# A written order for the first layer's cross-attention and shared expert, on all engines and over eight PSUM banks in turn

## The chip, the cores and the metric

The kernel runs on one core of a Trainium2 chip. A core has five engines that run side by side, each taking its own instructions strictly in the order in which they are queued: TensorE (PE: matrix multiplications and transposes; its weight loads are shown as PEld), VectorE (DVE), ScalarE (ACT), GpSimd (POOL) and SyncE (SP, which here only starts DMA transfers). They work on an on-chip memory, SBUF, and TensorE writes its results to a second one, PSUM, of eight banks, from which DVE or ACT read them. Engines wait for each other by semaphores. The metric is the time of one execution on the device in microseconds (us), median of three runs.

## The reference, cut to what matters

The reference is a two-layer decoder in float32 on 64 sequences of 64 positions with 128 features. Each layer has self-attention, cross-attention with a context of the same shape, and a feed-forward network of experts. The change lies in the first layer's cross-attention and in the part of its expert network that follows at once. Cut to that:

```
# x: 64 x 64 x 128; context: the same shape; 16 heads of 64
lat = layer_norm(layer_norm(x)) * g2 + b2       # x is normalised outside too
ctx = layer_norm(context) * g1 + b1
q   = lat @ Wq;   k, v = split(concat([ctx, lat], axis=1) @ Wkv)
w   = softmax(q k^T / 8)                        # 64 queries, 128 keys, 16 heads, per sequence
x   = x + (w v) @ Wout

h      = layer_norm(x)
probs  = softmax(rms_norm(h) @ router_w.T)      # 8 experts, the best two are taken
routed = each expert's silu(h rg) * (h ru) @ rd on at most 640 of its rows, weighted, added back
shared = (silu(h @ sg) * (h @ su)) @ sd         # 1024 hidden features, all rows
x      = x + shared + routed
```

## The kernel before

The 4096 rows are held in SBUF as eight tiles `xres[g]` of 128 partitions by 4 by 128 (a group g is eight sequences). The program has four stages, each with its own pools of SBUF and PSUM: the first layer's self-attention and dense experts (A), the stage of this change (X), the eight routed experts of the first layer one after the other (B), and the second layer (C).

**Stage X for a group.** The context rows are loaded by SP into `cg` (`load`, L912). `latent_rows` and `context_rows` normalise the rows: statistics on DVE (`ln_stats`, L154 and L155), the inverse root as a power on POOL (`inv_sqrt`, L163), a subtraction and multiplication for each 128 rows on DVE (L175). The latents go through two roots, since they are normalised twice. `keys_by_feature` transposes four tiles of 128 by 128 on TensorE (`transpose4`, L67) and ACT scales them into `kvT`; `keys_by_row` transposes back into `kvN`. Query and key weights are folded beforehand into `wqk`, value and output weights into `wvo`, so that `queries` makes for two heads of four sequences a piece of `qx` from the latents (matmuls `xq`, ACT copy L960), and `scores` multiplies the queries of eight heads of one sequence with its keys (matmuls `sc`, four products of 128 by 128 in one bank). The softmax: DVE takes the negative maximum and adds it (L976, L978), ACT the exponential (L979), DVE the sum and its reciprocal (L981, L982), POOL the multiplication (L983). `keys_first` transposes the result (`pt_p`) and ACT copies it to `pT` (L990); `sums` weights the keys' rows with it (`pu`, copied to `uT` by ACT, L1004); `output` adds 16 heads' products with `wvo` for two sequences (`pz`) and DVE adds them to `xres` (L1017). So a group has 16 pieces each of `queries`, `scores`, `keys_first` and `sums`, and four of `output`.

Then `ffn_rows` normalises the new rows into `xf`, `ffn_features` transposes them into `xfT`, `ffn_route` computes the router's logits (`rl`), the two best experts and their weights in some twenty small DVE operations, and the running count of rows for each expert; `ffn_places` turns these, with a matmul over earlier rows (`pp`), into the row's place in a DRAM table, `sidx`. `dispatch` scatters 128 rows to that table by two indirect DMAs on POOL's queue (L1097), one for each chosen expert. `shared` makes 128 of the shared expert's 1024 hidden features (matmuls `gg_s` and `gu_s`, tanh on ACT L1118, two DVE operations L1119 and L1120 into `sh`), eight pieces for a group, and `shared_out` multiplies 128 rows with `sd` (`sp`) and adds them to `xres` (L1133).

**What sets the order.** `at(slot, place, f, ...)` enters a piece in a list; `run_todo` calls all pieces by slot and place and, while it runs, `mm` and `transpose` keep TensorE's instructions in that order. In stages A and C `eng.pin()` does the same for DVE, ACT and POOL, and slots come from long tables of times written in the code. In stage X the slots are eight to a group (one for each sequence, with twelve places in each), in a regular pattern: scores of sequence b one slot before its transposes and sums, the next group's queries six slots ahead, the routed part of a group in the slots after its last output. Only TensorE is held to this order there; the instructions of DVE, ACT and POOL are put in an order by the framework's scheduler, and so is each of them against the others.

**Banks and buffers.** `psum_pool(pa, "psX", mm=3, sc=2, tp=1, av=2)` gives stage X three banks for queries, outputs, shared pieces and the router, two for scores, one for all transposes and two for `sums`. With `turns=True`, as in stage A, banks of a kind are taken strictly in turn. Buffers in SBUF that matter: `cg` 1, `p` (the softmax tile) 3, `pT` 2, `uT` 2, `qx` 2, `kvT` 2, `sh` 3, `th` 2.

**The stage's end.** Stage B's first load (`rg`, L1181) and its rows `xe` (L1188, read from the scattered table) stand on SP's queue.

Of the kernel before, what the change touches and what calls it, by code (L numbers as in the profile page):

```python
# [7 lines left out]
F32 = mybir.dt.float32  # L8
# [8 lines left out]
P = 128  # L17
D = 128
# [36 lines left out]
def decoder(ctx: ExitStack, tc: tile.TileContext, io: dict, out: bass.AP):  # L55
# [123 lines left out]
    def transpose4(src, nm):  # L179
        n = min(src.shape[1], TG)  # L180
        pt = psum("tp" if "tp" in banks else "mm", [P, TG, P], f"pt_{nm}")[:, 0:n]
        for i in range(n):
            transpose(pt[:, i, :], src[:, i, :], ident)
        return pt
# [714 lines left out]
    with ExitStack() as pa:  # L899
        psum_pool(pa, "psX", mm=3, sc=2, tp=1, av=2)  # L900
# [5 lines left out]

        run = sm.tile([P, E1], F32, tag="run", name="run")
        nc.vector.memset(run, 0.0)
# [4 lines left out]

        def latent_rows(s):

            g, x4 = s.g, xres[s.g]
            mv = ln_stats(sm, x4, f"l{g}")
            r = inv_sqrt(sm, mv[:, :, 1], EPS, f"l{g}")
            v2 = var_after(sm, mv[:, :, 1], r, f"l{g}")
            r2 = inv_sqrt(sm, v2, EPS, f"l2{g}")  # L920
            nc.vector.tensor_tensor(out=r2, in0=r2, in1=r, op=ALU.mult)
            s.ll = fk.tile([P, TG, D], F32, tag="ll", name=f"ll_{g}")
            normalise(s.ll, x4, mv, r2)

        def context_rows(s):
            g = s.g
            mv = ln_stats(sm, s.cg, f"c{g}")
            r = inv_sqrt(sm, mv[:, :, 1], EPS, f"c{g}")
            s.cn = fk.tile([P, TG, D], F32, tag="cn", name=f"cn_{g}")
            normalise(s.cn, s.cg, mv, r)  # L930

        def keys_by_feature(s, k):

            if k:
                s.kvT = fk.tile([P, 8, 2, S], F32, tag="kvT", name=f"kvT_{s.g}", bufs=2)
            pt = transpose4(s.ll if k else s.cn, f"{'l' if k else 'c'}{s.g}")
            nc.scalar.activation(
                s.kvT[:, :, k, :],
                split_b(pt),
                AF.Identity,  # L940
                scale=lnv[:, 2 * k : 2 * k + 1],
                bias=lnv[:, 2 * k + 1 : 2 * k + 2],
            )

        def keys_by_row(s, h):

            if h == 0:
                s.kvN = fk.tile([P, 8, D], F32, tag="kvN", name=f"kvN_{s.g}", bufs=2)
            pt = transpose4(s.kvT[:, 4 * h : 4 * h + 4].rearrange("p b c t -> p b (c t)"), f"n{s.g}_{h}")
            nc.scalar.copy(s.kvN[:, 4 * h : 4 * h + 4, :], pt)  # L950

        def queries(s, hg, h):

            if h == 0:
                s.qx[hg] = big.tile([P, 4, 16, S], F32, tag="qx", name=f"qx_{s.g}_{hg}", bufs=2)
            lat = s.kvT[:, 4 * hg : 4 * hg + 4, 1, :]
            pq = psum("mm", [P, 2, 4, S], f"xq_{s.g}_{hg}_{h}")
            for j in range(2):
                mm(pq[:, j], lhsT=wqk[:, h + j, :], rhs=lat, start=True, stop=True)
            nc.scalar.copy(s.qx[hg][:, :, h : h + 2, :].rearrange("p b h q -> p h b q"), pq)  # L960

        def scores(s, b, hf):
# [3 lines left out]
            psc = psum("sc", [P, 4, P], f"sc_{nm}")  # L966
            for j in range(4):
# [6 lines left out]
                )  # L974
            nmx = sm.tile([P, 4], F32, tag="nmx", name=f"nmx_{nm}", bufs=4)
            nc.vector.tensor_reduce(out=nmx, in_=psc, axis=AX, op=ALU.max, negate=True)  # L976
            pr = wk.tile([P, 4, P], F32, tag="p", name=f"p_{nm}", bufs=3)
            nc.vector.tensor_tensor(out=pr, in0=psc, in1=bcast(nmx, P), op=ALU.add)  # L978
            nc.scalar.activation(pr, pr, AF.Exp, scale=0.125)  # L979
            rc = sm.tile([P, 4], F32, tag="rc", name=f"rc_{nm}", bufs=4)  # L980
            nc.vector.tensor_reduce(out=rc, in_=pr, axis=AX, op=ALU.add)  # L981
            nc.vector.reciprocal(rc, rc)  # L982
            nc.gpsimd.tensor_tensor(out=pr, in0=pr, in1=bcast(rc, P), op=ALU.mult)  # L983
            s.pr[b, hf] = pr

        def keys_first(s, b, hf):
            nm = f"{s.g}_{b}_{hf}"
            pt = transpose4(s.pr[b, hf], f"p{nm}")
            s.pT[hf] = wk.tile([P, 4, P], F32, tag="pT", name=f"pT_{nm}", bufs=2)
            nc.scalar.copy(s.pT[hf], pt)  # L990

        def sums(s, b, hf):

            if b % 2 == 0 and hf == 0:
                s.uT[b // 2] = wk.tile([P, 16, 2, S], F32, tag="uT", name=f"uT_{s.g}_{b // 2}")
            pu = psum("av", [P, 8, S], f"pu_{s.g}_{b}_{hf}")
# [3 lines left out]
                rhs=s.pT[hf].rearrange("p j t -> p (j t)"),  # L1000
# [3 lines left out]
            nc.scalar.copy(s.uT[b // 2][:, 8 * hf : 8 * hf + 8, b % 2, :], pu)  # L1004

        def output(s, i):
            pz = psum("mm", [P, D], f"pz_{s.g}_{i}")
# [9 lines left out]
            nc.vector.tensor_tensor(out=xt, in0=pz, in1=xt, op=ALU.add)  # L1017

        def ffn_rows(s):
            g, x4 = s.g, xres[s.g]  # L1020
            mv = ln_stats(sm, x4, f"f{g}")
            r = inv_sqrt(sm, mv[:, :, 1], EPS, f"f{g}")
            s.xf = io_p.tile([P, TG, D], F32, tag="xf", name=f"xf_{g}")
            normalise(s.xf, x4, mv, r)
            s.rr = inv_sqrt(sm, var_after(sm, mv[:, :, 1], r, f"f{g}"), EPS32, f"f2{g}")

        def ffn_features(s):
            pt = transpose4(s.xf, f"f{s.g}")
            s.xfT = fk.tile([P, TG, P], F32, tag="xfT", name=f"xfT_{s.g}", bufs=2)
            nc.scalar.copy(s.xfT, pt)  # L1030

        def ffn_route(s):

            g = s.g
            ts_ = slice(TG * g, TG * g + TG)
            pl = psum("mm", [P, TG, E1], f"rl_{g}")
            for i in range(TG):
                mm(pl[:, i, :], lhsT=s.xfT[:, i, :], rhs=rwT, start=True, stop=True)
            lg = sm.tile([P, TG, E1], F32, tag="lg", name=f"lg_{g}")
            nc.vector.tensor_tensor(out=lg, in0=pl, in1=bcast(s.rr, E1), op=ALU.mult)  # L1040
            e = exp_shifted(sm, lg, E1, f"f{g}")
            top = sm.tile([P, TG, 2], F32, tag="top", name=f"top_{g}")
            nc.vector.tensor_reduce(out=top[:, :, 0], in_=e, axis=AX, op=ALU.max)
            oh1 = first_max(sm, e, top[:, :, 0], E1, f"f1{g}")
            nc.vector.scalar_tensor_tensor(e, oh1, -2.0, e, ALU.mult, ALU.add)
            nc.vector.tensor_reduce(out=top[:, :, 1], in_=e, axis=AX, op=ALU.max)
            oh2 = first_max(sm, e, top[:, :, 1], E1, f"f2{g}")
            tot = sm.tile([P, TG], F32, tag="tot", name=f"tot_{g}")
            nc.vector.tensor_tensor(out=tot, in0=top[:, :, 0], in1=top[:, :, 1], op=ALU.add)
            nc.vector.reciprocal(tot, tot)  # L1050

            nc.vector.tensor_scalar(tot, tot, 0.5, None, ALU.mult)
            nc.vector.tensor_tensor(out=wtop[:, ts_, :], in0=top, in1=bcast(tot, 2), op=ALU.mult)

            s.oh = (oh1, oh2)
            s.msk = sm.tile([P, TG, E1], F32, tag="msk", name=f"msk_{g}")
            nc.vector.tensor_tensor(out=s.msk, in0=oh1, in1=oh2, op=ALU.add)
            s.before = sm.tile([P, TG, E1], F32, tag="before", name=f"before_{g}")
            nc.vector.tensor_copy(s.before[:, 0, :], earlier[0])
            for i in range(TG - 1):  # L1060
                nc.vector.tensor_tensor(
# [3 lines left out]
            nc.vector.tensor_tensor(out=run, in0=s.before[:, TG - 1, :], in1=s.msk[:, TG - 1, :], op=ALU.add)  # L1065
            earlier[0] = run

        def ffn_places(s):

            g = s.g  # L1070
            ts_ = slice(TG * g, TG * g + TG)
            pp = psum("mm", [P, TG, E1], f"pp_{g}")
            mm(pp, lhsT=cst[:, C_ST : C_ST + P], rhs=s.msk, start=True, stop=False)
            mm(pp, lhsT=ones, rhs=s.before, start=False, stop=True)
            kp = sm.tile([P, TG, E1], F32, tag="kp", name=f"kp_{g}")
            nc.vector.tensor_scalar(kp, pp, float(CAP), None, ALU.is_lt)
            sl = sm.tile([P, TG, E1], F32, tag="sl", name=f"sl_{g}")
            nc.vector.tensor_tensor(
# [3 lines left out]
            nc.vector.tensor_tensor(out=sl, in0=sl, in1=bcast(tr, E1), op=ALU.subtract)  # L1082
            nc.vector.tensor_tensor(out=sl, in0=sl, in1=kp, op=ALU.mult)
            for k, oh in enumerate(s.oh):
                nc.vector.tensor_tensor(out=oh, in0=oh, in1=sl, op=ALU.mult)
                si = sm.tile([P, TG], F32, tag="si", name=f"si_{g}_{k}")
                nc.vector.tensor_reduce(out=si, in_=oh, axis=AX, op=ALU.add)
                nc.vector.tensor_tensor(out=si, in0=si, in1=tr, op=ALU.add)
                nc.vector.tensor_copy(sidx[:, ts_, k], si)
                nc.vector.tensor_scalar(si, si, float(NSLOT), None, ALU.min)  # L1090
                nc.vector.tensor_copy(gidx[:, ts_, k], si)
# [15 lines left out]
        def shared(s, c):  # L1107

            if c % 4 == 0:
                s.hid[c // 4] = big.tile([P, 4, 512], F32, tag="hid", name=f"sh_{s.g}_{c // 4}", bufs=3)  # L1110
            rhs = s.xfT.rearrange("p i t -> p (i t)")
            pg = psum("mm", [P, 512], f"gg_s{s.g}_{c}")
            mm(pg, lhsT=sg[:, c * P : (c + 1) * P], rhs=rhs, start=True, stop=True)
            pu = psum("mm", [P, 512], f"gu_s{s.g}_{c}")
# [3 lines left out]
            nc.scalar.activation(th, pg, AF.Tanh, scale=0.5)  # L1118
            nc.vector.scalar_tensor_tensor(th, th, 1.0, pg, ALU.add, ALU.mult)  # L1119
            nc.vector.tensor_tensor(out=s.hid[c // 4][:, c % 4, :], in0=th, in1=pu, op=ALU.mult)  # L1120

        def shared_out(s, i):
            pe = psum("mm", [P, D], f"sp_{s.g}_{i}")
# [9 lines left out]
            nc.vector.scalar_tensor_tensor(xt, pe, 0.5, xt, ALU.mult, ALU.add)  # L1133


        (X_S0, X_Q0, X_T0, X_S1, X_G, X_T1, X_U0, X_Q1, X_U1, ONE_T, X_Z, ONE_M) = range(12)
        earlier = [run]
        for g in range(NG):
            s = Group()
            s.g, s.qx, s.pr, s.pT, s.uT, s.hid = g, {}, {}, {}, {}, {}  # L1140
            t = 8 * g
            at(t - 12, X_S0, load, s)
            at(t - 10, X_G, latent_rows, s)
            at(t - 9, X_G, context_rows, s)
            at(t - 8, ONE_T, keys_by_feature, s, 1)
            at(t - 7, ONE_T, keys_by_feature, s, 0)
            at(t - 6, ONE_T, keys_by_row, s, 0)
            at(t - 5, ONE_T, keys_by_row, s, 1)
            for hg in range(2):
                for h in range(0, 16, 2):  # L1150
                    at(t - 6 + 4 * hg + h // 4, X_Q1 if h % 4 else X_Q0, queries, s, hg, h)
            for b in range(8):
                for hf, (sc, tr, su_) in enumerate(((X_S0, X_T0, X_U0), (X_S1, X_T1, X_U1))):
                    at(t + b - 1, sc, scores, s, b, hf)
# [1058 lines left out]
```

## Time and profile before

| what | value |
|---|---|
| time, median of 3 runs | 1911.66 us (1910.52 to 1919.04) |
| profiled execution | 1925.23 us, span 1923.5 us |
| mean granted TensorE clock | 0.976 |
| busy in the span | PE 95%, PEld 72%, DVE 64%, ACT 50%, POOL 30% |
| stage X, first context statistics to last shared output | about 442 to 1177 us |
| stage B's first TensorE instruction | 1183.09 us |

Times in the trace are microseconds from the start of the span. A line of TensorE gives the start, the length, the operation and its tiles, how many instructions were merged (x), and in brackets how long the engine stood idle before it and what ended that. A matmul in float32 shows as two instructions. A TensorE piece's length includes the time until its last result has drained; the next piece starts before that, so the difference of two starts tells what a piece costs. Idle time of the other engines costs nothing where TensorE is not made to wait.

### The profile page before, as it was taken

To read this page: it belongs to the slowest core of one execution; us is meant where nothing else is said; L and a number is where in the kernel's file an instruction comes from. 1 tells how busy PE (TensorE), PEld (TensorE's weight loads), DVE (VectorE), ACT (ScalarE), POOL (GpSimd) and SP (SyncE) were. 2 spreads that over 40 slices of the span, in tenths; PEclk is the share of its full clock that TensorE was granted. 3 is DMA by queue.
4 is the path that set the end of the run, shared out by engine and by line. 5 is a ranking of instruction groups with operands and counts; after the bars stand their busy time and mean duration, and the time that the engine had idled before them with its cause. 6 is when DMAs were issued, how large, how long until landed. Compare 5 with 4: busy or idle time off the path is not lost.

```text
span 1923.5 us, 42409 instructions
## 1 busy us (share of the span) xinstructions
PE 1833.8 (95%) x17390; PEld 1378.1 (72%) x17390; DVE 1224.6 (64%) x3492; ACT 959.2 (50%) x1743; POOL 586.4 (30%) x600
## 2 busy tenths in 40 slices
PE   8999999997999999999999998998999999999998
PEld 6666667676877777777878775774777776777775
DVE  5566666636675766666556754554587687676678
ACT  2444444444554454445454432335577666666553
POOL 1111111102234242423223231006575554543332
PEclk9799999998999999999999998998899999999999
DMA  8000000000000000000000002321000100100000
GB/s 284 16 2 2 1 2 2 2 1 17 7 6 12 6 12 9 9 12 6 6 2 4 1 3 83 109 62 33 20 13 13 18 16 16 17 9 8 8 2 18
DMA packets 39791, 41.67 MB, mean 22 GB/s; under 512 B 4501, under 2 KB 31445, under 8 KB 39340
## 3 DMA queue, kind: packets, MB, share of 16 engines
q1 hardware_dynamic: 29100, 27.40, 4.6%
q0 software_dynamic: 4096, 6.83, 1.6%
q10 hardware_dynamic: 6400, 4.72, 0.8%
q8 instruction: 137, 2.24, 0.5%
q14 instruction: 58, 0.48, 0.1%
HBM read 28.97 MB, written 11.53 MB: 21 GB/s over the span
## 4 chain that ended last, share of the span: by engine, by line
PE 78%; DVE 11%; issue 4%; POOL 2%; ACT 2%; DMA 1%; ACTq 0%; SPq 0%; POOLq 0%; DVEq 0%
PE sc L64 6%; PE pz L64 6%; PE pu L64 5%; PE xq L64 5%; PE down L64 5%; PE ph L64 5%; PE py L64 3%; PE xqT L64 3%; PE pt_p L67 2%; DVE x L80 2%; PE xz L64 2%; PE sp L64 2%; PE ey L64 2%; PE gg_s L64 2%; PE gu_s L64 2%
## 5 line engine op out<-in xcount | busy, mean ns | idle before, releaser
L983 POOL TENSOR_TENSOR p<-p,rc 128x512 f32<-128x512 f32 x128 | 133.2, 1044 | 297.2 <-DVE rc L982 100.2
L64 PEld LDWEIGHTS down<-w2T,hid 128*128 128x128 f32 x1024 | 129.5, 191 | 44.9 <-DVE x L80 21.6
L960 ACT COPY qx<-xq 128x512 f32<-128x512 f32 x128 | 74.6, 583 | 159.1 <-PE xq L64 158.7
L80 ACT ACTIVATE hid<-ph,wa 128x512 f32<-128x512 f32 x128 | 85.7, 686 | 135.3 <-PE ph L64 135.0
L64 PE MATMUL down<-w2T,hid 128*128 128x128 f32 x1024 | 139.7, 279 | 2.5 <-DVE x L80 2.0
L64 PE MATMUL pu<-pT,kvN 128*128 128x512 f32 x256 | 131.8, 598 | 6.3 <-ACT pT L990 6.2
L64 PE MATMUL sc<-kvT,qx 128*128 128x128 f32 x1024 | 136.4, 276 | 0.0
L64 PE MATMUL ph<-hT,w1T 128*128 128x512 f32 x256 | 133.1, 618 | 0.1
L64 PE MATMUL xq<-kvT,wqk 128*128 128x256 f32 x512 | 132.6, 384 | 0.6
L64 PEld LDWEIGHTS sc<-kvT,qx 128*128 128x128 f32 x1024 | 125.4, 192 | 4.5 <-issue 2.6
L64 PEld LDWEIGHTS pz<-wvo,uT 128*128 128x128 f32 x1024 | 118.4, 192 | 9.1 <-issue 6.2
L64 PEld LDWEIGHTS xq<-kvT,wqk 128*128 128x128 f32 x512 | 93.4, 193 | 37.0 <-issue 25.8
L64 PE MATMUL pz<-wvo,uT 128*128 128x128 f32 x1024 | 119.5, 275 | 0.0
L976 DVE TENSOR_REDUCE nmx<-sc 128x4 f32<-128x512 f32 x128 | 88.0, 687 | 48.9 <-PE sc L64 47.9
L1323 POOL DMA_INDIRECT yk<-y_dram,gidx x64 | 65.3, 1021 | 150.6 <-DMA y_dram<-ye 134.3
L990 ACT COPY pT<-pt_p 128x512 f32<-128x512 f32 x128 | 74.2, 580 | 69.5 <-PE pt_p L67 68.7
L979 ACT ACTIVATE p<-p 128x512 f32<-128x512 f32 x128 | 80.7, 631 | 45.8 <-DVE p L978 33.9
L1097 POOL DMA_INDIRECT xg_dram<-xf,sidx x64 | 63.7, 995 | 121.0 <-DVE si L1090 47.5
L80 POOL TENSOR_TENSOR p_x<-p_x,nmx_x 128x512 f32<-128x512 f32 x64 | 65.4, 1043 | 99.9 <-DVE nmx_x L80 96.9
L80 DVE SCALAR_TENSOR_TENSOR x<-ey,oh_e,x 128x128 f32<-128x128 f32 x256 | 88.8, 348 | 9.4 <-PE ey L64 2.1
L1017 DVE TENSOR_TENSOR x<-pz,x 128x128 f32<-128x128 f32 x32 | 9.3, 292 | 132.8 <-PE pz L64 132.8
L981 DVE TENSOR_REDUCE rc<-p 128x4 f32<-128x512 f32 x128 | 87.0, 680 | 8.7 <-ACT p L979 6.4
(327 smaller groups left out, 4255.0 us busy)
## 6 DMA issues: line engine op xcount, KB each, us to landing
xg_dram<-zero SPq DMA_DIRECT2D x10, 256.0 KB, 7.1
xe<-xg_dram SPq DMA_DIRECT2D x8, 320.0 KB, 3.7
y_dram<-ye ACTq DMA_DIRECT2D x8, 320.0 KB, 3.8
x<-in_x SPq DMA_DIRECT2D x8, 256.0 KB, 12.1
cg<-in_ctx SPq DMA_DIRECT2D x8, 256.0 KB, 2.8
rg<-in_rg SPq DMA_DIRECT2D x8, 256.0 KB, 2.8
rd<-in_rd SPq DMA_DIRECT2D x8, 256.0 KB, 3.2
ru<-in_ru ACTq DMA_DIRECT2D x8, 256.0 KB, 2.7
```

The lines of the kernel that those rows point to most:

```text
L64: return in_order(nc.tensor.matmul(*args, **kwargs))
L67: return in_order(nc.tensor.transpose(*args))
L80: return lambda *args, **kwargs: in_order(getattr(self.engine, name)(*args, **kwargs))
L960: nc.scalar.copy(s.qx[hg][:, :, h : h + 2, :].rearrange("p b h q -> p h b q"), pq)
L976: nc.vector.tensor_reduce(out=nmx, in_=psc, axis=AX, op=ALU.max, negate=True)
L979: nc.scalar.activation(pr, pr, AF.Exp, scale=0.125)
L981: nc.vector.tensor_reduce(out=rc, in_=pr, axis=AX, op=ALU.add)
L983: nc.gpsimd.tensor_tensor(out=pr, in0=pr, in1=bcast(rc, P), op=ALU.mult)
L990: nc.scalar.copy(s.pT[hf], pt)
L1017: nc.vector.tensor_tensor(out=xt, in0=pz, in1=xt, op=ALU.add)
L1097: nc.gpsimd.indirect_dma_start(out=xg_dram[:, :], out_offset=bass.IndirectOffsetOnAxis(ap=sidx[:, TG * s.g + i, k : k + 1], axis=0), in_=s ...
L1323: nc.gpsimd.indirect_dma_start(out=yk, out_offset=None, in_=y_dram[:, :], in_offset=bass.IndirectOffsetOnAxis(ap=gidx[:, TG * s.g + i, k : ...
```

## The change

Stage X gets what stages A and C have. `eng.pin()` is called, so the instructions of DVE, ACT and POOL are held to the written order too. The pieces are cut smaller: `latent_rows` and `context_rows` lose their statistics and roots to `sums_of`, `context_sums`, `root_of` and `second_root`; `scores` is cut into `scores` (matmuls), `shift`, `exp` and `whole`; `ffn_route` into `ffn_logits`, `ffn_exp`, `ffn_route` and `ffn_masks`; `ffn_places` into `ffn_places` (matmuls) and `ffn_slots`; `shared` into `shared` and `shared_mul`. The eight slots of a group become two tables of times: one with a period of 8 for the groups in the middle, one piece by piece for the start (group 0 and the start of 1) and for the end (group 7 and the end of 5 and 6). All eight PSUM banks become one kind, taken in turn. The instructions themselves, their shapes, the weights and the SBUF buffers stay.

```diff
-        psum_pool(pa, "psX", mm=3, sc=2, tp=1, av=2)
+        psum_pool(pa, "psX", turns=True, bank=8)
...
+        eng.pin()
+        V, A, G = eng.vector, eng.scalar, eng.gpsimd
...
+        def context_sums(s):
+            for i in range(TG):
+                sums_of(s, "c", i)
+
+        def root_of(s, nm):
+            st, mv = s.ln[nm]
+            s.ln[nm] = (mv, inv_sqrt(sm, mv[:, :, 1], EPS, f"{nm}{s.g}"))
...
+        def shift(s, b, hf):
...
+            V.tensor_reduce(out=nmx, in_=psc, axis=AX, op=ALU.max, negate=True)
+            pr = wk.tile([P, 4, P], F32, tag="p", name=f"p_{nm}", bufs=3)
+            V.tensor_tensor(out=pr, in0=psc, in1=bcast(nmx, P), op=ALU.add)
+            s.pr[b, hf] = pr
+
+        def exp(s, b, hf):
+            pr = s.pr[b, hf]
+            A.activation(pr, pr, AF.Exp, scale=0.125)
+
+        def whole(s, b, hf):
...
+            V.tensor_reduce(out=rc, in_=pr, axis=AX, op=ALU.add)
+            V.reciprocal(rc, rc)
+            G.tensor_tensor(out=pr, in0=pr, in1=bcast(rc, P), op=ALU.mult)
...
-            t = 8 * g
-            at(t - 12, X_S0, load, s)
-            at(t - 10, X_G, latent_rows, s)
...
+        for when, lo, hi, f, *args in (
...
+            (2.36, 1, 6, whole, 3, 1),
+            (2.4, 1, 6, exp, 4, 1),
+            (2.44, 1, 6, whole, 3, 0),
+            (2.48, 1, 6, whole, 4, 1),
+            (2.52, 1, 6, sums, 2, 1),
+            (2.6, 1, 6, keys_first, 3, 1),
...
+            (5.0, 0, 6, keys_first, 6, 0),
+            (5.16, 0, 6, sums, 6, 0),
...
+            (9.96, 0, 5, ffn_features),
+            (10.28, 0, 5, ffn_logits),
...
+            (11.8, 0, 5, ffn_places),
+            (12.0, 0, 5, ffn_slots),
+            (12.76, 0, 5, dispatch, 0),
+            (13.12, 0, 5, dispatch, 1),
+            (13.56, 0, 5, dispatch, 2),
...
+            (17.28, 0, 4, dispatch, 3),
...
+        ):
+            for g in range(lo, hi + 1):
+                at(0, round(8 * g + when, 4), f, who[g], *args)
...
+            (-1.306, 0, root_of, "l"),
+            (-1.305, 0, context_sums),
+            (-1.304, 0, second_root, "l"),
+            (-1.303, 0, root_of, "c"),
+            (-1.302, 0, latent_rows),
...
+            (56.612, 5, dispatch, 3),
...
+            (56.615, 7, whole, 6, 1),
...
+            (56.646, 7, ffn_features),
+            (56.647, 6, shared_mul, 6),
+            (56.648, 7, second_root, "f"),
+            (56.649, 6, dispatch, 3),
+            (56.65, 6, shared_mul, 7),
+            (56.651, 7, ffn_logits),
...
+            (56.658, 7, ffn_places),
+            (56.659, 7, shared_mul, 0),
+            (56.66, 7, ffn_slots),
```

## The prediction

> **What bounds the kernel now.** I read the page's chain first, then windows by stage, then TensorE's instructions in order of time inside the changed stage, then the queues at its end. The chain that ended last, by engine:
>
> ```profile
> PE 78%; DVE 11%; issue 4%; POOL 2%; ACT 2%; DMA 1%; ACTq 0%; SPq 0%; POOLq 0%; DVEq 0%
> ```
>
> TensorE carries it, so the changed stage (first query 451.66 us, last scatter 1173.16 us) can only gain what TensorE loses there. The windows (second column the stretch, then busy us of PE, PEld, DVE, ACT, POOL, then the granted clock):
>
> ```profile
> core 0: us, PE busy (x) PEld busy (x) DVE busy (x) ACT busy (x) POOL busy (x), PEclk, DMA share, GB/s
> 100.00:200.00 100.00, 98.84 (x1004) 68.92 (x1004) 62.12 (x184) 48.55 (x70) 12.02 (x15) 1.00 0.01 1
> 440.00:460.00 20.00, 11.66 (x51) 9.52 (x50) 12.03 (x71) 5.56 (x9) 6.04 (x6) 0.74 0.09 27
> 730.00:820.00 90.00, 88.28 (x544) 69.45 (x544) 58.39 (x175) 42.98 (x79) 29.44 (x30) 1.00 0.03 10
> 1500.00:1600.00 100.00, 96.36 (x1441) 72.46 (x1440) 70.68 (x193) 64.21 (x126) 54.46 (x53) 1.00 0.10 17
> ```
>
> The reader is to see that the stage's steady part (730 to 820) already keeps PE busy 98.1%, while the two stages whose order is already written for all engines stand at 98.8% (100 to 200, attention) and 96.4% (1500 to 1600, second layer): a written order is not by itself better. DVE has 31.6 us of 90 free, ACT 47, POOL 60. TensorE's own order shows what is lost:
>
> ```profile
> 709.18 3.74 PE L64 MATMUL pz<-wvo,uT 128*128 128x128 f32 x32
> 712.75 1.06 PE L64 MATMUL sc<-kvT,qx 128*128 128x128 f32 x8
> 713.65 1.03 PE L64 MATMUL xq<-kvT,wqk 128*128 128x256 f32 x4
> 714.51 0.60 PE L67 MATMUL pt_p<-cst,p 128*128 128x128 f32 x4
> 714.95 1.06 PE L64 MATMUL sc<-kvT,qx 128*128 128x128 f32 x8
> ...
> 718.00 1.02 PE L64 MATMUL pu<-pT,kvN 128*128 128x512 f32 x2
> 718.86 1.03 PE L64 MATMUL xq<-kvT,wqk 128*128 128x256 f32 x4
> ...
> 720.58 0.60 PE L67 MATMUL pt_f<-cst,xf 128*128 128x128 f32 x4
> 721.91 0.66 PE L67 MATMUL pt_c<-cst,cn 128*128 128x128 f32 x4 [0.73 <-ACT xfT L1030]
> 722.40 1.06 PE L64 MATMUL sc<-kvT,qx 128*128 128x128 f32 x8
> ...
> 728.81 1.13 PE L64 MATMUL xq<-kvT,wqk 128*128 128x256 f32 x4
> 730.85 1.12 PE L64 MATMUL pu<-pT,kvN 128*128 128x512 f32 x2 [0.91 <-ACT pT L990]
> 731.81 0.38 PE L67 MATMUL pt_n<-cst,kvT 128*128 128x128 f32 x2
> ```
>
> Differences of starts are the true price of a piece: output 3.57, scores 0.89, query pair 0.86, four transposes 0.44, weighted sum 0.86. Between the two bracketed waits everything runs at that pace; at them 1.33 stands for 0.44, and 2.04 for 0.86.
>
> ```profile
> 1173.16 0.97 POOL L1097 DMA_INDIRECT xg_dram<-xf,sidx  x1 [1.40 <-DMA xg_dram<-xf,sidx]
> 1175.40 0.34 SPq L1181 DMA_DIRECT2D rg<-in_rg  x1
> 1176.35 0.43 SPq L1188 DMA_DIRECT2D xe<-xg_dram  x1
> 1183.09 1.09 PE L67 MATMUL pt_xe<-cst,xe 128*128 128x128 f32 x4 [6.18 <-DMA xe<-xg_dram]
> ```
>
> The next stage waits for the last of eight scatters of group 7 (one every 2.37 us: 0.97 to issue, 1.40 for the one before), then 10 us of loads; TensorE, done at 1176.9, idles 6.2. So the end of the stage is set by when group 7's places are known (pp, done 1154.04; first scatter 1155.95, 1.9 later).
>
> **The work that stays.** No instruction is added or removed; every count is the same. A group's TensorE work, by those differences: 16 scores 14.2, 16 query pairs 13.9, 21 sets of transposes 9.2, 16 sums 13.8, 4 outputs 14.3, 8 shared pieces of 1.72 13.8, 4 shared outputs of 1.79 7.1, logits 0.8 and places 0.4: 87.4 us. A period measured between the same wait (730.85 to 820.96) is 90.11. The 2.7 us between are nearly all in the two places: 0.9 at the first, 0.3 before and 1.2 at the second, 0.2 of restarts. Over the stage: 8 x 87.4 = 699.2, less 0.9 for the first two transposes (before 451.66) and 22.8 after pp leaves 675.5. It takes 451.66 to 1154.04, 702.4. So 26.9 us is all there is to win before the scatters.
>
> **Part by part.** *Head.* In the table group 0's context statistics stand between the two roots of its latent rows. The context load is issued at 441.80 and takes 2.8, so lands at 444.6; DVE waits for it, statistics 1.1, three small operations 0.6, second root on POOL from 446.6 (before 445.37) to 447.6, the context's root behind it to 448.6. Latent rows (1.25) end at 449.0, context rows at 450.1, first query 450.6 to 450.7 against 451.66: 1.0 gained. What is queued behind DVE's wait is only group 0's own start. The clock stays low there (window 440 to 460: 0.74): eight query matmuls take 3.62 at 451.66 and 1.89 at 455.92, a loss of 1.7 that stays. In the head the first softmax chain needs, by rows: shift 0.69 + 0.68, exp 0.63, sum and reciprocal 0.85, POOL 1.04, hand-overs 0.5: 4.4; but DVE is given group 1's start between (statistics 1.5, roots 0.8 and a POOL wait of 1.0, rows 1.25). Against 7.4 us of TensorE work the first transposes are late by 0.8, those of (0,1) by 1.2. Head: 1.7 + 2.0 + 0.2 = 3.9 of loss.
>
> *Steady groups.* Both waits go: the routed features' transposes are followed by a shared output and more (4.0 us of TensorE work before the logits, where the copy needs 0.8), and pT's copies (0.83 from transposes to sums) have at least 0.87 between. What is late next: I set pieces by hand along the table for group 3. DVE keeps up through its densest stretch (10.3 us of DVE work in 10.0 of PE, around the places): it is back on time when the next scores end. One set, transposes (3,1), follows three sums of exponentials in a row and is late by about 0.5. Transposes (6,0) to sums (6,0) have 0.04 to spare, so a copy late by 0.2 costs 0.2.
>
> *Banks.* A bank is written again eight allocations later. The tightest steady pair, scores (5,0) then sums (4,1), has 4.7 us of PE work between, and the shift that frees it needs 0.3 + 1.4. Cost nothing, covered by 3 us; if DVE lags by more, TensorE pays the excess. The three buffers of p, two of pT, two of qx are unchanged.
>
> *POOL.* Scatters, roots and multiplications now stand in one fixed order. A pair of scatters holds POOL 0.97 + 1.40 + 0.97 = 3.34 us; queued behind it are multiplications, for which transposes on PE wait. Group 3, multiplication (7,0) behind the second pair: ready 305.8 on an axis of PE work, done 306.9, transposes at 312.2: no cost. In the last group, group 5's fourth pair stands before multiplication (6,1): about 1.2 late.
>
> *SP.* The context loads move by some us within 45 of room; nothing else is on that queue until 1175. Cost nothing.
>
> *Tail.* Group 7's logits follow its features' transposes directly: 0.85 late. The routing chain (logits' scaling, exp 0.6, choice 2.9, masks 1.1, behind two shared multiplications) has 5.2 us of PE work to hide in and needs 6.2: 1.0 late. One shared multiplication (1.37) stands before the slots, so the first scatter comes 2.9 after places, not 1.9. Tail: 1.2 + 0.85 + 1.0 = 3.1, and 1.0 more before the scatters.
>
> *The unknown, E*: what six groups lose in all that I do not see. Lower end 0; upper end the second layer's rate, 2.4 idle per 100 us (its windows from 1400 to 1800) with restarts at the ratio of now (2.7 lost for 1.64 idle): 640 x 0.024 x 1.6 = 25. The attention stage's 1.2 per 100 gives 8 idle. My walk gives 0.5 a group, 3. I take 7, nearest the attention stage, which like this one is full of wide matmuls.
>
> [...] DVE's `ve` on 128x4 takes 0.15 us alone and up to 1.05 beside a POOL multiplication. [...]
>
> **Sum**, against the profiled execution (1925.23 us, span 1923.5): 450.7 + 675.5 + 3.9 + 3.1 + 7 = 1140.2 for the places against 1154.04: 13.8 sooner, less 1.0: scatters, loads and all behind them 12.8 sooner. 1912.4 us. The median of the runs shown, 1911.66, is 0.993 of the profiled time: 1899.
>
> **Rivals.** (1) *The waits only move*: the removed 2.7 a group comes back as waits for POOL or DVE somewhere else; E = 18 to 25. For it: 96.4% in the second layer. Against: own chains all fit. Time 1925.2 - 1.8 to + 5, or 1910 to 1917. (2) *PE never waits in the steady part*: E about 0, 1892. For it: the walk. Against: no stage here does so for long. (3) *Slower: scatter pairs hold up the softmax.* Place: POOL, multiplications behind dispatch. If each of 32 pairs delays transposes by the full wait for the scatter before (1.40), 45 us are lost against 19.8 won: 1925.2 + 25 = 1950, or 1937. It decides above 0.9 us a pair. Against: 5 us to spare where I looked.
>
> **Numbers.** About 0.5% (9.6 us) is what a measurement here can tell from no change. Forecast case (E 3 to 10) 0.45, rival 2 0.17, rival 1 and its neighbours 0.26, rival 3 0.12. Faster 0.62, same 0.26, slower 0.12. Range 1891 to 1915: from rival 2 with a milder tail to rival 1 at E = 24; it leaves out rival 3 and little more.
>
> **What would show it.** Right: first query near 450.7; the waits of pt_c for xfT and of pu for pT gone; period 87.5 to 88.7; places near 1140; scatters 2.37 apart from about 1143; TensorE still idle some 6 us before the next stage. Wrong: pt_p waiting for POOL p, or sc for a bank held by DVE, several times a group; a period above 90.

## The result, and the profile after

The changed kernel takes 1924.3 us (median of 9 runs, 1922.17 to 1926.74) where the kernel before, beside it, takes 1915.1 (median of 9, 1910.52 to 1919.18). The ratio is 1.005, 95% interval 1.0035 to 1.0065: it is slower by 0.5%. The prediction was 1899.

The profiled execution (1923.78 us, span 1921.7) can be set against the median as it stands, which the one of before could not. The last product of stage A (`down`), the same code in both, starts at 440.57 us in the trace of before and at 431.06 in this one. So times in the stage are counted from that instruction. From it to stage B's first TensorE instruction before needs 742.5 us, the changed kernel 748.5: the stage itself is 6.0 us longer. From the first query to the last places it is 701.3 against 707.8.

The chain that ended last, by engine (before it was PE 78%, DVE 11%):

```profile
PE 76%; DVE 14%; issue 5%; POOL 3%; DMA 1%; ACT 1%; ACTq 0%; SPq 0%; POOLq 0%; DVEq 0%
```

The windows of the start and of the steady part (columns as above):

```profile
440.00:460.00 20.00, 18.95 (x103) 16.16 (x103) 12.96 (x45) 13.16 (x22) 5.07 (x5) 0.93 0.05 14
730.00:820.00 90.00, 87.57 (x540) 68.75 (x539) 62.30 (x174) 43.36 (x78) 29.59 (x29) 1.00 0.03 10
```

PE is busy 87.57 of 90 where before had 88.28: the steady part got worse, though DVE still has 27.7 us free. TensorE's order there, in the group whose places come at 741.38:

```profile
725.04 1.06 PE L64 MATMUL sc<-kvT,qx 128*128 128x128 f32 x8
...
728.10 1.95 PE L64 MATMUL sp<-sd,sh 128*128 128x128 f32 x16
729.89 3.74 PE L64 MATMUL pz<-wvo,uT 128*128 128x128 f32 x32
...
736.05 1.13 PE L64 MATMUL sc<-kvT,qx 128*128 128x128 f32 x8 [0.70 <-DVE p L80]
...
742.68 1.95 PE L64 MATMUL sp<-sd,sh 128*128 128x128 f32 x16
744.47 1.06 PE L64 MATMUL sc<-kvT,qx 128*128 128x128 f32 x8
...
752.29 0.63 PE L67 MATMUL pt_p<-cst,p 128*128 128x128 f32 x4 [1.53 <-DVE p L80]
```

The two waits of before (for `xfT`, for `pT`) are gone. In their place stand two for DVE's `p`, in every group. By the written order the first is scores (5,0), the second transposes (5,1), and neither needs that `p` as data: each wants the bank, eight allocations on, that scores (4,0) (725.04) and scores (6,0) (744.47) still hold until DVE's shift has read them. What DVE did meanwhile:

```profile
725.56 0.69 DVE L80 TENSOR_TENSOR sh<-gth_s,gu_s 128x512 f32<-128x512 f32 x1
730.09 0.29 DVE L80 SCALAR_TENSOR_TENSOR x<-sp,x 128x128 f32<-128x128 f32 x1 [3.85 <-PE sp L64]
730.30 0.18 DVE L80 TENSOR_REDUCE mx_f<-lg 128x4 f32<-128x32 f32 x1
...
733.95 0.17 DVE L80 TENSOR_TENSOR wtop<-top,tot 128x8 f32<-128x8 f32 x1
...
734.46 0.66 DVE L80 TENSOR_REDUCE nmx<-sc 128x4 f32<-128x512 f32 x1
735.22 0.69 DVE L80 TENSOR_TENSOR p<-sc,nmx 128x512 f32<-128x512 f32 x1
...
744.67 0.29 DVE L80 SCALAR_TENSOR_TENSOR x<-sp,x 128x128 f32<-128x128 f32 x1 [2.29 <-PE sp L64]
744.87 0.18 DVE L80 TENSOR_SCALAR kp<-pp 128x32 f32<-128x32 f32 x1
...
751.45 0.69 DVE L80 TENSOR_TENSOR p<-sc,nmx 128x512 f32<-128x512 f32 x1
```

The reader is to see a queue, not a lack of time. Scores (4,0) are done at about 726, and DVE falls idle at 726.2; but next in its written order is the addition of a shared output, whose matmuls TensorE has yet to run (3.85 us idle), and behind that the whole choice of experts (730.30 to 734.1). Only then comes shift (4,0), done at 735.9, ten microseconds after its scores. The same happens again 10 us later: the places are there at 742, but the slots stand behind the next shared output's addition (2.29 idle), and shift (6,0), behind the slots, ends at 752.1.

A period, measured between two groups' places, is 90.77 (before 90.10; TensorE's work 87.4).

### The profile page after: what moved, and what is told of

Read it like the earlier page. It is cut to its first block, busy times and chain, and to the rows that moved or that the text cites. A ratio compares the mean times of both kernels' runs of the same rounds, so it can differ in the third digit from the quotient of the medians.

```text
span 1921.7 us, 42393 instructions
## 1 busy us (share of the span) xinstructions
PE 1828.0 (95%) x17390; PEld 1375.3 (72%) x17390; DVE 1254.5 (65%) x3492; ACT 960.9 (50%) x1743; POOL 586.7 (31%) x600
## 4 chain that ended last, share of the span: by engine, by line
PE 76%; DVE 14%; issue 5%; POOL 3%; DMA 1%; ACT 1%; ACTq 0%; SPq 0%; POOLq 0%; DVEq 0%
PE sc L64 6%; PE down L64 5%; PE pz L64 5%; PE xq L64 5%; PE ph L64 5%; PE pu L64 5%; PE py L64 3%; PE pt_p L67 3%; PE xqT L64 3%; PE xz L64 3%; DVE x L80 2%; PE ey L64 2%; PE sp L64 2%; PE xkT L64 2%; PE gg_e L64 2%
## 5 line engine op out<-in xcount | busy, mean ns | idle before, releaser
L64 PE MATMUL xq<-kvT,wqk 128*128 128x256 f32 x512 | 128.5, 381 | 0.0
L80 ACT COPY uT<-pu 128x512 f32<-128x512 f32 x128 | 74.7, 585 | 77.9 <-PE pu L64 77.9
L80 DVE TENSOR_TENSOR p<-sc,nmx 128x512 f32<-128x512 f32 x128 | 88.5, 692 | 18.6 <-PE pt_p L67 7.6
L67 PEld LDWEIGHTS pt_p<-cst,p 128*128 128x128 f32 x512 | 61.1, 141 | 51.9 <-POOL p L80 30.1
L80 POOL TENSOR_TENSOR p_x<-p_x,nmx_x 128x512 f32<-128x512 f32 x64 | 65.4, 1044 | 100.5 <-DVE nmx_x L80 89.7
```

Source lines behind the costliest of these rows:

```text
L64: return in_order(nc.tensor.matmul(*args, **kwargs))
L67: return in_order(nc.tensor.transpose(*args))
L80: return lambda *args, **kwargs: in_order(getattr(self.engine, name)(*args, **kwargs))
```

## The experiments

Theory D, formed on this reading: VectorE's written order loses, since additions that wait for TensorE stand ahead of shifts, and the banks in turn carry the delay to TensorE. Theory B: eight banks in turn tie the engines together and lose by themselves, whatever the order. All ratios are to the kernel before, run beside; the median of before moved between 1911.7 and 1918.5 from set to set, so only ratios and the stage's length in the traces are compared. The length is given twice: "queries to places" is first query to last places (701.3 before, 707.8 changed), "stage" is from stage A's last product to stage B's first TensorE instruction (742.5 and 748.5).

**One shift earlier.** Shift (4,0) ahead of the shared output's addition.

```diff
-            (3.0, 1, 6, shift, 4, 0),
+            (2.78, 1, 6, shift, 4, 0),
```

> Theory D (VectorE's written order): in each group VectorE reaches shift (4,0) only after it has waited for a shared output and run the routing choice behind it, and scores (5,0) then wait for the bank that shift (4,0) holds (0.70 us in four of the traced groups, 0.31 in one). Moving that one shift ahead of the shared output's addition lets this wait go; its scores end about 8 us before it runs now. A group gets 0.8 us shorter (0.70 and a restart), six groups some 4 to 5 us: 1919 to 1920 against 1924. The wait of transposes (5,1), 1.53, stays. Theory B (eight banks in turn tie everything together): the wait turns up at the next user of a bank behind VectorE; period 90.6 to 90.8, 1923 to 1925.

The wait of scores (5,0) is gone, the other stays at 1.52; period 90.09; queries to places 703.6, stage 744.0, so 4.3 to 4.5 shorter. The time's ratio is 1.0056 (1.0033 to 1.0079): of these 4 us it shows nothing, and only the trace speaks here.

**One addition later.** The addition of shared output 0 behind the slots and `whole` (5,1).

```diff
-            (19.96, 0, 4, shared_out, 0),
+            (19.96, 0, 4, shared_out, 0, False),
+            (20.35, 0, 4, shared_add, 0),
```

> Theory D: VectorE stands 2.29 us at the addition of shared output 0 before it may start the slots, and everything behind (whole (5,1), shifts (6,1) and (6,0)) is that much later; transposes (5,1) wait 1.53 for the bank of scores (6,0). With the addition moved behind the slots and whole (5,1), shift (6,0) ends some 2.5 us sooner and this wait goes: 1.5 to 1.8 us a group, five groups with a shared output there, 7 to 9 us: 1915 to 1917 against 1924. The wait of scores (5,0), 0.70, stays. Theory B: the wait moves to another piece, 1922 to 1925.

The wait of transposes (5,1) is gone in the steady groups, that of scores (5,0) stays (0.71); period 89.17; queries to places 699.1, 8.7 shorter; ratio 1.0021 (1.0002 to 1.0040).

**Both.**

> Theory D: both waits go, the gains add: period 88.2 to 88.6 instead of 90.78, 11 to 13 us less than the changed kernel, 1911 to 1913, which is about 2 below before's median of 1915. Theory B: 1921 to 1925.

Period 88.49, queries to places 695.0: 12.8 shorter, nearly the sum of 4.3 and 8.7. Ratio 1.0000 (0.9979 to 1.0022). TensorE in the same place of the group, with both waits gone:

```profile
728.68 3.74 PE L64 MATMUL pz<-wvo,uT 128*128 128x128 f32 x32
...
733.12 1.02 PE L64 MATMUL pu<-pT,kvN 128*128 128x512 f32 x2
733.98 1.05 PE L64 MATMUL sc<-kvT,qx 128*128 128x128 f32 x8
```

and DVE, with shift (4,0) now ahead of the addition:

```profile
724.66 0.69 DVE L80 TENSOR_REDUCE nmx<-sc 128x4 f32<-128x512 f32 x1 [1.25 <-PE sc L64]
725.45 0.69 DVE L80 TENSOR_TENSOR p<-sc,nmx 128x512 f32<-128x512 f32 x1
728.88 0.29 DVE L80 SCALAR_TENSOR_TENSOR x<-sp,x 128x128 f32<-128x128 f32 x1 [1.42 <-PE sp L64]
```

Two moved rows give back what the change lost. DVE still waits for `sp` at this addition (1.42 us, 3.85 before the move); what has changed is what stands behind it.

**The three other engines free again.**

```diff
-        eng.pin()
+        eng.unpin()
```

> TensorE's order, the banks and the loads as in the changed kernel; VectorE, ScalarE and GpSimd are again ordered by the scheduler. In the order that VectorE gets there, shift (4,0) stands ahead of the routing choice, and both additions of shared outputs stand behind the routing choice and the slots. Theory D: neither wait of TensorE on a bank of scores is left, period 87.8 to 88.8, 1909 to 1916. Theory B, or TensorE's new order being worse in itself: the period stays above 90 and the time at 1921 to 1927. If the written order of the other three engines was the gain, and not the loss, it is slower than the changed kernel, above 1927.

Neither wait is left. Four of the groups have 0.34 and 0.23 for DVE at two other places, three have 0.23 to 0.44 for POOL's `p`. Period 87.7 to 89.5, queries to places 690.9, stage 734.4; ratio 0.9978 (0.9952 to 1.0004). With the same order on TensorE, the written order of the other engines cost 16.9 us from queries to places and 14.1 of the stage.

**The banks alone, in the kernel before.**

```diff
     def psum(tag, shape, name):
+        tag = "bank" if "bank" in banks else tag
...
-        psum_pool(pa, "psX", mm=3, sc=2, tp=1, av=2)
+        psum_pool(pa, "psX", turns=True, bank=8)
```

> The kernel before, with nothing changed but its banks: all tiles of the stage in PSUM take eight banks in turn instead of kinds (3, 2, 1 and 2). TensorE's order stays that of before, the other engines are ordered by the scheduler. Theory D: the turn costs nothing by itself as long as VectorE comes to its shifts in time; within 3 us of before (1909 to 1916 if before is at 1912), the period between logits 89.5 to 90.3, since the wait of a tile's transposes for the one spare bank may go. Theory B: the turn is what loses, the time 5 us or more above before, with new waits of TensorE for VectorE.

Ratio 0.9995 (0.9979 to 1.0011), stage 741.6, periods 89.7 with one of 91.4 (there two pieces of TensorE, `pt_n` and `pz` from 811.86 us on, took 5.60 us, a group earlier 4.01). The wait of the context's transposes is gone; that of `pu` for `pT` is 1.89 instead of 0.91; no wait for VectorE inside a group.

```profile
721.12 1.13 PE L64 MATMUL pu<-pT,kvN 128*128 128x512 f32 x2 [1.89 <-ACT pT L991]
```

Theory B falls: turns cost nothing where DVE comes in time. The opposite case, the changed kernel's order with banks by kind, was not run, so what part of its loss fixed kinds would have kept away stays open.

**VectorE alone free.**

```diff
         eng.pin()
+        eng.vector = nc.vector
```

> The changed kernel with ScalarE and GpSimd still held in the written order and VectorE alone ordered by the scheduler. Theory D (it is VectorE's order): as fast as the run in which all three were free, or within 4 us of it, 1908 to 1913; the waits of scores (5,0) and transposes (5,1) for VectorE are gone. Rival (the order of ScalarE or GpSimd loses as well): it stays above 1917, half way to the changed kernel or worse.

Ratio 0.9987 (0.9971 to 1.0003), periods 90.0 to 91.0, queries to places 699.7, stage 738.9. By the times this is as good as three free engines (0.9978), as Theory D had it. In the traces it is not: it gives back 9.6 of their 14.1 us of the stage and 8.2 of their 16.9 from queries to places, and the steady period hardly moves. The waits of scores (5,0) and transposes (5,1) are gone, but output 1 now waits for DVE, 1.15 to 2.21 a group. DVE's line where it is late, and POOL's lines before it:

```profile
671.79 0.16 DVE L943 TENSOR_TENSOR rs_2l<-rs_2l,rs_l 128x4 f32<-128x4 f32 x1 [5.84 <-POOL rs_2l L80]
```

```profile
668.68 1.01 POOL L1141 DMA_INDIRECT xg_dram<-xf,sidx  x1 [0.46 <-DMA xg_dram<-xf,sidx]
669.72 1.05 POOL L80 TENSOR_TENSOR p<-p,rc 128x512 f32<-128x512 f32 x1
670.72 1.04 POOL L80 TENSOR_TENSOR rs_2l<-ve_2l,cst 128x4 f32<-128x4 f32 x1
```

The scheduler put the latent rows early on DVE, POOL's written order has the root they need behind several scatters, and DVE stands 5.84 us. It is the same fault with other engines: two orders that do not fit each other. So that DVE's order is what loses is shown by the two moved rows, not by this run.

**The written order made to fit.** The two edits, and 17 moves of rows by a few places (shift (4,0) once more among them, so 18 rows differ from the changed kernel); some of them:

```diff
-            (0.04, 1, 6, sums, 0, 0),
+            (0.34, 1, 6, sums, 0, 0),
-            (2.08, 1, 6, keys_first, 2, 1),
+            (2.18, 1, 6, keys_first, 2, 1),
-            (4.4, 1, 6, shift, 6, 1),
+            (4.54, 1, 6, shift, 6, 1),
-            (5.16, 0, 6, sums, 6, 0),
+            (5.26, 0, 6, sums, 6, 0),
...
-            (-1.2261, 1, context_sums),
+            (-1.2845, 1, context_sums),
-            (-1.1721, 1, second_root, "l"),
+            (-1.2848, 1, second_root, "l"),
...
-            (56.596, 5, shared_out, 0),
+            (56.5945, 5, shared_out, 0),
-            (56.66, 7, ffn_slots),
+            (56.6585, 7, ffn_slots),
```

> The run with both edits, and 17 more rows of the table moved by a few places, chosen by walking along the order with the durations of these traces so that no engine waits for a piece ahead of one that another engine needs: in the steady groups sums (0,0), transposes (2,1), sums (6,0), shift (6,1), shift (4,0) and one root; at the start group 1's context statistics and its root of latent rows, ahead of group 0's first softmax in the trace, go earlier, and three pieces of group 0; at the end seven pieces of groups 5 to 7, such as the last slots ahead of a shared multiplication. Theory D: with the written orders fitting one another the stage comes to the price of TensorE's work, period 87.4 to 88.0 against 88.5 with the two edits alone, first start and end some 8 us less: 10 to 17 us below the run with both edits, 0.5 to 0.9% below before. Rival (a written order is brittle, other waits come up as they did in the changed kernel): no more than 4 us below the run with both edits.

Ratio 0.9918 (0.9890 to 0.9946), the fastest version, faster than both kernels. Period 87.56 to 87.63, queries to places 683.4, stage 724.8. That is 10.9 us of the stage below the run with both edits, as expected. TensorE is never idle in the steady part:

```profile
730.00:820.00 90.00, 90.00 (x559) 71.76 (x558) 66.47 (x178) 45.35 (x83) 29.56 (x29) 1.00 0.03 10
```

**Those rows with the three engines free.** The last kernel, with `eng.unpin()` for `eng.pin()`.

> The same rows, but VectorE, ScalarE and GpSimd ordered by the scheduler again, so that only TensorE's order and the loads are those of the run before it. Theory D: what counts is that the orders fit one another; the scheduler does not know the written times, so it comes out like the first run with three free engines, 0 to 0.5% below before, and slower than the one with the rows held on all engines. Rival (TensorE's order alone makes the gain): as fast as that one, within 3 us.

Ratio 0.9929 (0.9904 to 0.9953), stage 730.4. The expectation failed: it is not slower than the run with all engines held by an amount that the times show, and its stage is 4.0 us shorter than in the first run with free engines (ratio 0.9978). In the traces the held order is still ahead, by 5.6 us of the stage; its periods are even, those of this run go from 89.20 down to 87.15. So of the 17.7 us by which the fastest stage is shorter than before's, 8.1 are there with the changed kernel's order on TensorE and free engines, 4.0 come with the moved rows and 5.6 with holding the other engines to them. Some of the moved rows are pieces of DVE, which the scheduler is then handed in another order, so the 4.0 are not shown to be TensorE's alone.

**How late VectorE may be.** In the fastest version, behind the slots of groups 0 to 4, additions that nobody reads; five, then fourteen.

```diff
+            if g < 5:
+                idle = sm.tile([P, TG, E1], F32, tag="idle", name=f"idle_{g}")
+                for _ in range(5):
+                    V.tensor_tensor(out=idle, in0=s.msk, in1=sl, op=ALU.add)
```

> The rows of the fastest run so far, and behind the slots of groups 0 to 4 five more small VectorE additions that nobody reads (about 0.22 us each by the rows beside them, 1.1 us a group). In that run's trace shift (6,0), behind the slots, frees the bank of its scores at about 739.4 and transposes (5,1) take it at 740.89: a cover of some 1.3 us after the hand-over. Theory D: 1.1 us is covered, the period stays at 87.6 to 87.9, the time within 2 us of that run. Rival (any VectorE work in these groups comes through to TensorE): 5 to 6 us slower.

> The same with fourteen additions, 3.1 us a group. Theory D: 1.3 is covered and the rest, 1.8 and a restart of 0.2, is paid by TensorE in each of five groups, at transposes (5,1), as a wait for VectorE: period 89.4 to 89.9, time 8 to 11 us above the run without them. Rival (VectorE, idle for a third of each period, takes 3.1 us more in its idle time): the time stays within 3 us.

Five: periods 87.56 to 87.62, ratio 0.9914 (0.9880 to 0.9949), nothing paid. Fourteen, 3.1 us of work a group: ratio 0.9980 (0.9958 to 1.0002), and the stage is 13.3 us longer than without them, more than the 8 to 11 expected. The second and third group have a period of 89.7 and so pay 2.1. The first pays 3.9; it has no cover, since TensorE waits 1.36 there without any addition. The fourth pays 3.8 with the same waits as its neighbours, but three pieces behind them, from 839.52 to 843.43 us, took 0.69, 1.71 and 1.51 us, a group earlier 0.49, 0.86 and 0.86: the other 1.7. The fifth pays 1.4. VectorE, which in the version without them is idle for a quarter of the window (23.5 of 90 us), still hands on two thirds of what is added in the groups where nothing else disturbs. The place was expected one allocation too late: TensorE waits first at a shared piece, for the bank of the shared output whose addition stands behind the slots, then at the transposes for POOL's product:

```profile
743.40 3.12 DVE L80 TENSOR_TENSOR idle<-msk,sl 128x32 f32<-128x32 f32 x14
747.96 1.12 PE L64 MATMUL gu_s<-xfT,su 128*128 128x512 f32 x2 [0.94 <-DVE x L80]
749.74 0.44 PE L67 MATMUL pt_p<-cst,p 128*128 128x128 f32 x2 [0.65 <-POOL p L80]
```

## Why the prediction was wrong, step by step

**Right.** *Head*: first query 1.0 sooner; counted from stage A's last product it came after 10.05 us instead of 11.09; the low clock that was to cost 1.7 there cost 0.8 (5.58 us up to the first scores, 4.74 by the prices of the pieces; the granted clock was 0.71 from 441.11 to 443.67 us, then 1.00, and in the trace of before 0.50 from 451.66 to 455.92). *Both old waits go*: they did. *POOL*: no steady group waits behind a pair of scatters, so rival 3 is out; the one wait for POOL's `p` there, 0.2, is that of transposes (3,1) behind three sums in a row on DVE (0.5 said). But the premise, scatters in one fixed order with the rest, does not hold: multiplications and roots keep the written order in the trace, the scatters do not. All eight of group 0 are issued from 567 to 588 us, the last two eight multiplications and more ahead of their place in the table. *Tail*: logits 0.67 late (0.85 said), stage B still waits 6.4 for its rows. *VectorE beside POOL*: the sum has no term for small operations of VectorE that take longer beside POOL (`ve`, up to 1.05 us in the trace of before), and it needed none. In the changed kernel's steady part (730 to 820 us) the small ones with two inputs took 0.13 to 0.20 us each. A longer one is real (in the fastest version one `sl` took 0.98 from 732.90 on, while POOL's product ran from 732.79 to 733.83; 0.19 in the changed kernel's steady part), but from 630 to 990 us of that version it is about two a group (`ve_2f` 0.96 on average, `sl` 0.78 and 0.41).

**Wrong: "DVE keeps up ... back on time when the next scores end".** The step counted DVE's work, 10.3 us in 10.0, and not its waits. An addition of a shared output stands in DVE's queue where its piece stands in the order, but it can run only when TensorE has finished that piece. So the choice of experts and the slots could not start before 730.3 and 744.9, however free DVE was. In the trace of before DVE waits at such additions too, even longer in all (from 640 to 1000 us: 19.0 for `sp` and 71.3 for `pz`, against 35.4 and 21.0 in the changed kernel). The sum of such waits does not decide; what is queued behind them does. Two of the pieces behind them were enough: moving one shift and one addition took 12.8 us off the stage. In group 0 no such wait is needed: no shared output stands there, DVE works from 552.74 to 572.4 with one pause of 0.46, and transposes (5,1) still wait 1.84 for the bank, so there it is the work itself that stands ahead of the shift. The moved rows do not cure that; in the fastest version DVE works without a pause of note from 554.5 to 573.0, and TensorE waits

```profile
567.37 0.66 PE L67 MATMUL pt_p<-cst,p 128*128 128x128 f32 x4 [1.36 <-DVE p L80]
```

**Wrong: "Banks ... cost nothing, covered by 3 us".** The cover was there (9.25 us of TensorE work after scores (4,0), 5.24 after scores (6,0), by the order and the prices of the pieces), but the shift that frees a bank was taken to run 0.3 + 1.4 after its scores, and ran 10 and 7 after. The prediction's own condition, "if DVE lags by more, TensorE pays the excess", was what happened, and the two runs with added work measure it in the fitted order: 1.1 us covered, of 3.1 two thirds paid where nothing else disturbs.

**E.** 7 was taken for what could not be seen. First query to the end of the last places was to be 689.5 (1140.2 less 450.7) and came out at 708.8 (1149.89 less 441.11; the lengths given with the experiments end at the start of the places, a microsecond earlier), so E was 26 with the other terms as forecast, just beyond the upper end of 25 (27 with the 0.8 of the clock in the head). The two waits are 12.8 of the 19.3 us missed. The rest is at the start, where transposes wait for POOL's `p` five times (1.05 and 1.23 at the two places foreseen with 0.8 and 1.2, and 1.65 more by 545 us that were not) and once 1.84 for a bank, and in the last groups: 1.10 for `p` at 1077, and 1.90 + 0.21 for group 6's places, behind a shift and another shared output's addition, which the prediction did not look at. The 1.2 foreseen there for group 5's fourth pair of scatters did not come, since that pair was issued at 1034 and 1038, long before; the 1.10 at 1077 is a multiplication whose sum on DVE (1075.12) stood behind the rows of `xf`.

**The rivals.** Rival 1 (the waits only move, E 18 to 25) is what happened, a little worse than its end, and it had 0.26 with "its neighbours". Its argument against, "own chains all fit", was the error: each chain was fitted alone, against TensorE, and not behind what stands before it on its own engine. Rival 3 had the right form on the wrong engine. With the order made to fit, the steady part does what rival 2 said (PE never waits).

**The scale.** The sum was turned into a median with 0.993, the ratio of median to profiled time. That the long execution was long for a reason outside the stage could be read: windows of before and of the changed kernel over the same code of stage A, 20 to 50 and 50 to 100 us,

```profile
20.00:50.00 30.00, 25.98 (x431) 19.89 (x430) 18.99 (x52) 8.97 (x15) 4.66 (x5) 0.82 0.89 286
50.00:100.00 50.00, 47.49 (x501) 32.67 (x500) 28.43 (x84) 21.04 (x31) 5.28 (x8) 0.80 0.01 2
```

```profile
20.00:50.00 30.00, 26.57 (x520) 20.37 (x520) 24.20 (x69) 10.14 (x17) 6.08 (x7) 1.00 0.90 294
50.00:100.00 50.00, 48.08 (x456) 31.52 (x457) 30.26 (x92) 22.59 (x33) 5.67 (x7) 0.90 0.01 2
```

show a granted clock of 0.82 and 0.80 against 1.00 and 0.90: 9.5 us. It is a constant of that execution and not a factor. For the forecast it made little difference (12.8 less than the median is 1899 as well).

**Open.** The median is 9.2 us above before's, the stage in the traces only 6.0; in the first four runs, which were one set, the time is 4 to 9 us longer than the stage's length makes it (with both edits the stage is 6.8 shorter than before's and the ratio 1.0000), while for the last six the two agree within about 2. The code behind the stage is the same everywhere and took 730.7 to 744.5 us in the twelve traces. In the 40 us that begin 160 us behind stage B's first instruction the mean granted clock was 0.74 with both edits, 0.82 in the changed kernel and 0.93 with five added operations, the shortest trace. Whether that is chance or follows from the order was not tried.

## What to carry to other kernels

When an engine is put into a written order, go through its queue as the engine does: for each instruction that waits for another engine, ask what stands behind it and who needs that. Work summed by time says little, and neither does idle time; an engine idle for 30% (here DVE, 27.7 of 90 us) can be the one that stops the bound engine through a buffer or bank it frees late. A written order is worth what its fit is worth: the same table cost 0.5% as it stood, nothing with two rows moved, and gained 0.8% with 18.

## What was not expected of the hardware

The granted TensorE clock differs between executions in code that is the same: on average 0.80 against 0.90 from 50 to 100 us (above), and 0.74 to 0.93 in the 40 us that begin 160 us behind stage B's first instruction, with PE busy 39.2 of 40 at 0.74. Early on such an average is made of two levels: in the trace of before 0.50 from 40 to 70 us and 1.00 from 75 to 100, in the changed kernel 0.50 from 50 to 60 and 1.00 from 60 to 100. Work without a pause did not raise it at once: in the trace of before TensorE works from 60.38 on without one,

```profile
60.38 1.12 PE L67 MATMUL pt_m<-cst,hn 128*128 128x128 f32 x4 [2.49 <-DVE hn L80]
...
64.09 5.47 PE L64 MATMUL ph<-hT,w1T 128*128 128x512 f32 x6
69.35 1.02 PE L67 MATMUL gwT<-cst,gw 128*4 128x128 f32 x4
```

and the clock is 0.50 from 60 to 70 us, with PE busy 9.61 of 10, and 0.98 from 70 to 75. Some 14 us of spread behind the stage, and 9.5 in front of it, are more than the change itself is worth: at this size the length of the stage in a trace tells more than one profiled time.
